# A transformer block in 3-term fp32r matmuls: the distances between the operands in SBUF are turned round

## The chip, the cores and the metric

The kernel runs on one core of one Trainium2 chip. The metric is the device time of one execution in microseconds (us), lower is better. The five engines of the core are called PE (matmul), with PEld for its weight loads, DVE (vector), ACT (scalar), POOL and SP; SP only issues transfers here.

SBUF, the memory that the engines work in, has 128 partitions; a tile has the same byte address in each of its partitions. A matmul on PE has two operands in SBUF: the weights, which are loaded into the array first and stay there, and the operand that then moves through it, column by column. This document calls *distance* the start address of the moving operand less the start address of the weights, taken modulo 256 bytes. A tile that lies "64 behind" another begins at an address 64 bytes higher, modulo 256.

## The reference: what is computed

One PixArt block on x of 16 x 256 x 256 (16 batches, 256 tokens, width 256), with 16 heads of width 16, a condition vector per batch and a context of 256 tokens per batch. Cut to what matters:

```python
shift_a, scale_a, gate_a, shift_m, scale_m, gate_m = split(silu(c) @ W_mod + b_mod, 6)
q, k, v = split(modulate(ln(x), shift_a, scale_a) @ W_qkv + b_qkv, 3)
x = x + gate_a * (softmax(q @ k.T * scale) @ v @ W_proj + b_proj)
q_c = ln(x) @ W_qc + b_qc
k_c, v_c = split(ln(context) @ W_kvc + b_kvc, 2)
x = x + softmax(q_c @ k_c.T * scale) @ v_c @ W_cproj + b_cproj
h = gelu(modulate(ln(x), shift_m, scale_m) @ W_mlp1 + b_mlp1)
x = x + gate_m * (h @ W_mlp2 + b_mlp2)
```

All inputs and the output are float32.

## The kernel before, in words

**Precision.** Nearly all products run in fp32r, a float32 read at reduced precision. So each factor is split into a high part and a rest, and a product is the sum of three matmuls: high by high, high by rest, rest by high. The two parts of a source stand in tiles `xTh` and `xTl` (four buffers each), those of the queries and keys in `qkh` and `qkl` before they are sent to their place.

**Units.** There are 32 units: a self attention and a cross attention for each batch. A unit makes its keys, queries and values, forms its scores, and projects the result. The heads of a unit stand in pairs, and `beat(n, k)` with k from 0 to 7 goes through one pair of heads for the unit n and, at the same time, for its neighbours. A beat calls `visit`, which issues

- `s_tile`: the scores of unit n+1 for the row maxima (tile `s`). The weights are 128 columns of the queries `u.q`, the moving operand is the keys `u.k`, 256 columns. DVE takes the maximum.
- `t_part`: the scores of unit n again, transposed (tile `st`). Here the weights are 128 columns of the keys and the moving operand is the queries. ACT takes the exponential of them.

Both run as pairs: one matmul on partitions 0 to 63 (0 to 62 for `s`), one on 64 to 127, side by side in the two halves of the array. The document calls such a half of the array a *lane*. Queries and keys of a unit lie in one tile `big` of which there are three, used in turn by the units; the queries come first, the keys `8 * N` floats and a gap of `APART` floats later.

**Projections between the scores.** `lane` and `lanes` fill each beat with twelve steps of two projections, one per lane: keys, queries, values or the output projection of other units. For keys and queries (`o.tok` false) the weights of the matmul are the weight matrix (`wself`, `wqc`, `wkc`) and the source `xT` moves; for values and output projections (`o.tok` true) the source stays and the matrix (`wtok`, `wvc`, `wcp`) moves.

**The product with the values** (`av_part`, tile `o`) is plain float32, four heads side by side in the columns of the array.

**The last stage.** After the units comes the MLP of 16 batches with matmuls over all 128 partitions: `mlp_first` and `mlp_ahead` (tile `ph`; weights W1 in `wself`, the source `xT..m` moves) and `mlp_second` (tiles `s` and `st`; the hidden `hh` or `hl`, in the buffers `qkh` and `qkl`, stays and W2, which takes the place of the third `big`, moves).

**What sets the order.** Every engine works in the program's order; the order is written out by hand in `beat` and in a table `E_` of steps and places. Transfers stand on SP's queue.

**Where tiles lie.** Two pools, `const` and `work`, lay tiles one behind the other as they are first named. A helper `gap(pool, n, name)` reserves n bytes that nothing uses, so that what is named after it moves up. These lines set the distances before:

```python
APART = 16
        if i == 2:
            gap(const, 64, "gap_w2")
wt = const.tile([P, 16 * H + 2 * APART], F32R, name="wself")
wtok = wt[:, 8 * H + 2 * APART:].rearrange("p (a h) -> p a h", h=H)
            if name == "k0":
                gap(work, 64, "gap_l")
```

Of the kernel before, what the change touches and what calls it, by code (L numbers as in the profile page):

```python
# [11 lines left out]
F32R = mybir.dt.float32r  # L12
# [4 lines left out]
P = 128  # L17
# [4 lines left out]
def pixart_block(  # L22
# [8 lines left out]
    B, N, H = x.shape  # L31
# [28 lines left out]
    const = ctx.enter_context(tc.tile_pool(name="const", bufs=1))  # L60
    work = ctx.enter_context(tc.tile_pool(name="work", bufs=2))
# [6 lines left out]
    def ps_gen(name, tag=None):  # L68


        if tag is None and ps_turn[0] is not None:
            ps_turn[0] ^= 1
            tag = (SHORT, LONG)[ps_turn[0]]
        tag = tag or SHORT
        return psum.tile([P, 512], F32, tag=tag, name=name, bufs=2)
# [9 lines left out]
    def gap(pool, n, name):  # L85

        pool.tile([P, n // 4], F32, tag=name, name=name, bufs=1)

    APART = 16
    big, qks = [], []  # L90
    for i in range(3):
        if i == 2:
            gap(const, 64, "gap_w2")
        t = const.tile([P, 16 * N + APART], F32R, name=f"big{i}")
        big.append(t[:, :16 * N].rearrange("p (s a n) -> p s a n", s=2, n=N))
        qks.append([t[:, c:c + 8 * N].rearrange("p (a n) -> p a n", n=N) for c in (0, 8 * N + APART)])
    vts = [const.tile([P, NT, NH, 32], F32, name=f"v{i}") for i in range(3)]
    wt = const.tile([P, 16 * H + 2 * APART], F32R, name="wself")
    wself = wt[:, :16 * H].rearrange("p (a h) -> p a h", h=H)
    wtok = wt[:, 8 * H + 2 * APART:].rearrange("p (a h) -> p a h", h=H)  # L100
    cb = const.tile([P, H], F32, name="cb")
    ones = cb[:8]
    DVE.memset(ones, 1.0)
# [266 lines left out]
    def transposed(src, name, scale=None, pool=False):  # L370

        o = Box()

        def place():
            o.ps = ps_gen(f"psT_{name}", SHORT)

        def turn(fs=range(KC)):
            if len(fs) == KC:
                place()
            for f in fs:  # L380
                for t in range(NT):
                    PE.transpose(o.ps[:, f * N + t * P:f * N + (t + 1) * P],
                                 src()[:, t, f * P:(f + 1) * P], ident)

        def high():
            hi = work.tile([P, KC, N], F32R, tag="xTh", name=f"xTh_{name}", bufs=4)
            lo = work.tile([P, KC, N], F32R, tag="xTl", name=f"xTl_{name}", bufs=4)
            o.xT = (hi, lo)
            if scale is None:
                ACT.copy(hi.rearrange("p k n -> p (k n)"), o.ps)  # L390
            else:
                for f in range(KC):
                    ACT.activation(hi[:, f], o.ps[:, f * N:(f + 1) * N], AF.Identity, scale=scale[f])

        def low():
            hi, lo = o.xT
            if scale is None:
                DVE.tensor_tensor(lo.rearrange("p k n -> p (k n)"), o.ps,
                                  hi.rearrange("p k n -> p (k n)"), ALU.subtract)
            else:  # L400
                for f in range(KC):
                    DVE.scalar_tensor_tensor(lo[:, f], o.ps[:, f * N:(f + 1) * N], scale[f],
                                             hi[:, f], ALU.mult, ALU.subtract)

        def full():
            o.y = work.tile([P, KC, N], F32, tag="y", name=f"y_{name}", bufs=1)
            if scale is None:
                ACT.copy(o.y.rearrange("p k n -> p (k n)"), o.ps)
            else:
                for f in range(KC):  # L410
                    ACT.activation(o.y[:, f], o.ps[:, f * N:(f + 1) * N], AF.Identity, scale=scale[f])

        def rest_pool():
            hi, lo = o.xT
            POOL.tensor_tensor(lo, o.y, hi, ALU.subtract)

        def low_pool():
            full()
            rest_pool()

        o.full, o.rest_pool, o.place = full, rest_pool, place
        o.parts = [turn, high, low]
        o.low_pool = low_pool
        o.turn, o.high, o.low = turn, high, low_pool if pool else low
        return o

    def mm3(dst, W, f, xT):

        n = 0
        for k in range(KC):  # L430
            for a, b in ((W[0], xT[0]), (W[0], xT[1]), (W[1], xT[0])):
                PE.matmul(dst, a[:, k, f * P:(f + 1) * P], b[:, k],
                          start=(n == 0), stop=(n == 3 * KC - 1))
                n += 1
# [40 lines left out]
    def to_stack(W, src, bias, dst, which, name):  # L475

        o = Box()
        lo_row = (2, 1)[which]  # L480

        o.W, o.src, o.tok, o.name = W, src, False, name

        def first():
            o.ps = ps_gen(f"ps_{name}", LONG)
            mm3(o.ps[:, 0:N], W, 0, src.xT)

        def third():
            mm3(o.ps[:, N:], W, 1, src.xT)

        def second():
            third()
            high()

        def high():
            o.hi = work.tile([P, KC, N], F32R, tag="qkh", name=f"h_{name}", bufs=3)
            for f in range(KC):
                ACT.activation(o.hi[:, f], o.ps[:, f * N:(f + 1) * N], AF.Identity, bias=bias[f])

        def low():  # L500
            if name == "k0":
                gap(work, 64, "gap_l")
            o.lo = work.tile([P, KC, N], F32R, tag="qkl", name=f"l_{name}", bufs=3)
            if name == "k0":
                gap(work, 192, "gap_mx")
            for f in range(KC):
                DVE.scalar_tensor_tensor(o.lo[:, f], o.ps[:, f * N:(f + 1) * N], bias[f], o.hi[:, f],
                                         ALU.add, ALU.subtract)

        def low_pool():  # L510
            o.lo = work.tile([P, KC, N], F32R, tag="qkl", name=f"l_{name}", bufs=3)
            y = work.tile([P, KC, N], F32, tag="y", name=f"y_{name}", bufs=1)
            for f in range(KC):
                ACT.activation(y[:, f], o.ps[:, f * N:(f + 1) * N], AF.Identity, bias=bias[f])
            POOL.tensor_tensor(o.lo, y, o.hi, ALU.subtract)

        def send(part, q=SP):

            row = (0, 3 - lo_row, lo_row)[part]
            q.dma_start(dst[row:row + 4 * 31 + 1:4].bitcast(F32), (o.hi if part < 2 else o.lo).bitcast(F32))  # L520

        o.send = send
        o.parts = [first, second, low]
        o.third = third
        o.low_pool = low_pool
        o.high, o.low = high, low
        o.send_high = lambda: [send(part) for part in range(2)]
        o.send_low = lambda: send(2)
        o.steps = [first, second]
        return o  # L530
# [799 lines left out]
```

## Time and profile before

| | |
|---|---|
| median of 3 runs | 729.45 us (729.22 to 731.1) |
| the profiled execution | 729.69 us |
| its span, from the first to the last instruction | 727.9 us |
| PE busy | 716.5 us (98%), 9007 matmuls |
| PEld busy | 594.5 us (82%) |
| DVE, ACT, POOL busy | 558.7, 556.6, 540.9 us (77, 76, 74%) |
| granted TensorE clock | 0.999 |

A matmul's recorded duration holds its way through the array, so that matmuls that follow each other overlap in time: a group's mean is 276 to 306 ns while the next one starts much sooner. What a matmul costs in a full stream is the time from its start to the start of the next one in its lane, its *pace*. It is read from the timeline. Both lanes together make a *slot*: two half-height matmuls or one over all partitions.

### The profile page before, as it was taken

The page shows a single profiled execution, that of the slowest core. Times are in us where ns is not written, and L with a number is a line of the kernel's source. Part 1 is how long each engine was busy: PE and PEld are TensorE (multiplying, and loading weights), DVE is VectorE, ACT ScalarE, POOL GpSimd, SP SyncE. Part 2 cuts the span into 40 slices and gives each one's busy share as a digit, 9 for nine tenths or more (in the row PEclk, how much of TensorE's full clock was granted, in tenths as well). Part 3 has the DMA queues.
Part 4 walks back from the last instruction along what each step waited for, and adds up shares of the span by engine and source line. Part 5 has one row for each costly group of instructions (what it writes and reads, how often), then busy time and mean ns, then how long its engine had stood idle before and what let it go on. Part 6 is the DMA issues. An engine that isn't in the chain of part 4 may idle for free.

```text
span 727.9 us, 22489 instructions
## 1 busy us (share of the span) xinstructions
PE 716.5 (98%) x9007; PEld 594.5 (82%) x9007; DVE 558.7 (77%) x876; ACT 556.6 (76%) x971; POOL 540.9 (74%) x533
## 2 busy tenths in 40 slices
PE   9999999999999999999999999999999999999997
PEld 8777777777777777777777787777679999999996
DVE  4878888788888888888878888778675777777743
ACT  5667888888888888888888888888767677666661
POOL 8455687887867777786786798998766888666561
PEclk9999999999999999999999999999999999999999
DMA  7364545545545555454546655455332322312122
GB/s 251 139 232 154 171 150 179 170 162 176 180 144 169 173 185 173 170 185 135 183 162 190 191 180 200 150 176 196 92 90 89 89 59 87 71 62 88 49 53 73
DMA packets 81388, 106.14 MB, mean 146 GB/s; under 512 B 16451, under 2 KB 44389, under 8 KB 81285
## 3 DMA queue, kind: packets, MB, share of 16 engines
q1 hardware_dynamic: 80180, 103.92, 43.7%
q8 instruction: 71, 1.16, 0.7%
q10 hardware_dynamic: 1104, 0.79, 0.4%
q14 instruction: 33, 0.26, 0.1%
HBM read 35.89 MB, written 8.98 MB: 62 GB/s over the span
## 4 chain that ended last, share of the span: by engine, by line
PE 90%; DMA 4%; DVE 3%; ACT 1%; issue 1%; POOL 1%; SPq 0%; ACTq 0%
PE s L51 17%; PE o L51 16%; PE st L51 14%; PE ph L51 12%; PE ps_q L51 4%; PE ps_kc L51 3%; PE ps_qc L51 3%; PE ps_k L51 3%; PE ps_v_c L51 3%; PE ps_P_s L51 3%; PE ps_v_s L51 2%; PE ps_P_c L51 2%; DVE mx L51 2%; PE psT_c L51 2%; PE psT_s L51 1%; PE psT_q L51 1%
## 5 line engine op out<-in xcount | busy, mean ns | idle before, releaser
L51 DVE TENSOR_REDUCE mx<-s 128x4 f32<-128x1024 f32 x252 | 307.8, 1221 | 88.7 <-PE s L51 85.4
L51 ACT ACTIVATE pt<-st 128x1024 f32<-128x1024 f32 x256 | 263.2, 1028 | 53.8 <-PE st L51 52.6
L51 PE MATMUL o<-pt,v 128*32 128x256 f32 x2048 | 137.0, 385 | 0.0
L51 PE MATMUL s<-big 63*128 63x256 f32 x1008 | 117.5, 306 | 2.2 <-DMA U_s<-oT 0.8
L51 PE MATMUL st<-big 64*128 64x256 f32 (+1 forms) x1040 | 108.3, 283 | 1.4 <-ACT pt L51 0.7
L51 PE MATMUL ph<-xTh_m,wself 128*128 128x256 f32 x512 | 99.5, 280 | 0.0
L51 PEld LDWEIGHTS s<-big 63*128 63x128 f32 x1008 | 77.6, 185 | 21.8 <-issue 9.1
L51 POOL TENSOR_TENSOR hl<-hf,hh 128x512 fp32r<-128x512 f32 x60 | 81.2, 1370 | 18.8 <-ACT hh L51 18.8
L51 PEld LDWEIGHTS st<-big 64*128 64x128 f32 (+1 forms) x1040 | 81.5, 186 | 4.8 <-ACT pt L51 2.1
L51 PEld LDWEIGHTS o<-pt,v 128*32 128x32 f32 x2048 | 53.4, 109 | 38.9
L51 PEld LDWEIGHTS ph<-xTh_m,wself 128*128 128x128 f32 x512 | 81.8, 188 | 1.2 <-issue 0.4
L51 PE MATMUL ph<-xTl_m,wself 128*128 128x256 f32 x256 | 70.9, 277 | 0.0
L51 ACT ACTIVATE hf<-ph,bT 128x256 f32<-128x256 f32 x112 | 47.1, 475 | 19.4 <-PE ph L51 19.2
L51 ACT ACTIVATE hh<-ph,bT 128x256 fp32r<-128x256 f32 x112 | 47.2, 477 | 18.9 <-PE st L51 8.0
L51 PEld LDWEIGHTS ph<-xTl_m,wself 128*128 128x128 f32 x256 | 48.2, 188 | 0.0
L51 PE MATMUL s<-big,hh 128*128 128x256 f32 x256 | 45.2, 277 | 0.0
L51 DVE TENSOR_SCALAR xn_m<-x,mv_m,rs_m 128x256 f32<-128x256 f32 x28 | 33.9, 1249 | 14.8 <-POOL rs_m L51 14.8
L51 POOL TENSOR_SCALAR xn_c<-c,mv_c,rs_c 128x256 f32<-128x256 f32 x32 | 38.9, 1226 | 1.7
L51 PE MATMUL st<-big,hh 128*128 128x256 f32 x224 | 39.5, 276 | 0.0
L51 POOL TENSOR_SCALAR xn_q<-x,mv_q,rs_q 128x256 f32<-128x256 f32 x31 | 37.7, 1226 | 1.7
L51 PEld LDWEIGHTS s<-big,hh 128*128 128x128 f32 x256 | 38.7, 188 | 0.0
L51 ACT COPY oT<-o 128x512 f32<-128x512 f32 x64 | 37.6, 587 | 1.4 <-PE o L51 1.4
(226 smaller groups left out, 2119.1 us busy)
## 6 DMA issues: line engine op xcount, KB each, us to landing
big<-h_kc SPq DMA_DIRECT2D x32, 256.0 KB
big<-h_qc SPq DMA_DIRECT2D x32, 256.0 KB
big<-h_k SPq DMA_DIRECT2D x31, 256.0 KB
big<-h_q SPq DMA_DIRECT2D x31, 256.0 KB
big<-l_k SPq DMA_DIRECT2D x16, 256.0 KB
big<-l_q SPq DMA_DIRECT2D x16, 256.0 KB
g<-gd SPq DMA_DIRECT2D x16, 256.0 KB
U_s<-oT SPq DMA_DIRECT2D x32, 128.0 KB
```

What stands on the lines that cost most here:

```text
L51: i = f(*a, **k)
```

## The change

Five places change, and all of them move tiles in SBUF; no instruction is added, taken away or moved. The two built programs have the same 12412 instructions, in the same order on every engine, with the same shapes and the same waits.

```diff
-    APART = 16
+    APART = 48
     for i in range(3):
         if i == 2:
-            gap(const, 64, "gap_w2")
+            gap(const, 192, "gap_w2")
         t = const.tile([P, 16 * N + APART], F32R, name=f"big{i}")
...
-    wt = const.tile([P, 16 * H + 2 * APART], F32R, name="wself")
+    wt = const.tile([P, 16 * H + 32], F32R, name="wself")
-    wtok = wt[:, 8 * H + 2 * APART:].rearrange("p (a h) -> p a h", h=H)
+    wtok = wt[:, 8 * H + 32:].rearrange("p (a h) -> p a h", h=H)
...
         def high():
+            if name == "s0":
+                gap(work, 128, "gap_x")
             hi = work.tile([P, KC, N], F32R, tag="xTh", name=f"xTh_{name}", bufs=4)
...
             if name == "k0":
-                gap(work, 64, "gap_l")
+                gap(work, 192, "gap_l")
```

The start addresses modulo 256, as both programs have them:

| tile | before | after |
|---|---|---|
| queries of `big` 0, 1, 2 | 160, 224, 96 | 160, 96, 224 |
| keys of `big` 0, 1, 2 | 224, 32, 160 | 96, 32, 160 |
| W2 (in `big` 2) | 96 | 224 |
| sources `xTh`, `xTl` | 96 | 224 |
| `wself` (W of self keys and queries, W1), `wqc`, `wkc` | 160 | 160 |
| `wtok` (W of self values and projection), `wvc`, `wcp` | 32 | 32 |
| `qkh`, `qkl` (hidden of the MLP) | 160 | 160 |
| exponentials `pt`; values `v` | 96; 160 and 32 | 96; 160 and 32 |

So the distances (moving less weights) become:

| matmuls | before | after |
|---|---|---|
| keys, queries, W1 (source moves) | 192 | 64 |
| values, output projections (matrix moves) | 192 | 64 |
| W2 (matrix moves) | 192 | 64 |
| `st` (queries move, keys stay) | 192 | 64 |
| `s` (keys move, queries stay) | 64 | 192 |
| `o` and the transposes | | as before |

Every tile that a matmul of fp32r reads begins at 32 modulo 64, before and after.

## The prediction

> **What bounds the kernel now.** I read the first page from the top, then the chain, then the groups with their shapes kept apart, and last the timeline. The page first:
>
> ```profile
> span 727.9 us, 22489 instructions
> PE 716.5 (98%) x9007; PEld 594.5 (82%) x9007; DVE 558.7 (77%) x876; ACT 556.6 (76%) x971; POOL 540.9 (74%) x533
> ...
> PEclk9999999999999999999999999999999999999999
> ...
> PE 90%; DMA 4%; DVE 3%; ACT 1%; issue 1%; POOL 1%; SPq 0%; ACTq 0%
> PE s L51 17%; PE o L51 16%; PE st L51 14%; PE ph L51 12%; PE ps_q L51 4%; PE ps_kc L51 3%; PE ps_qc L51 3%; PE ps_k L51 3%; PE ps_v_c L51 3%; PE ps_P_s L51 3%; PE ps_v_s L51 2%; PE ps_P_c L51 2%; DVE mx L51 2%; PE psT_c L51 2%; PE psT_s L51 1%; PE psT_q L51 1%
> ```
>
> PE is the bound at a full clock, and 90% of the chain that ended last is PE's. Of that the product `o` and the transposes (`psT`) are outside the change; the rest are fp32r matmuls whose distances turn. In the answer for waits, PE waits for nobody for long:
>
> ```profile
> PE s L51 <- DMA U_s<-oT: 0.8, 1, 0.8
> PE st L51 <- ACT pt L51: 0.7, 3, 0.4
> ```
>
> DVE and ACT wait for PE instead (last columns of the first two rows here, which come from the groups by shape; columns: busy us, mean ns of one, idle before and its releaser):
>
> ```profile
> L51 DVE TENSOR_REDUCE mx<-s 128x4 f32<-128x1024 f32 x252 | 307.8, 1221 | 88.7 <-PE s L51 85.4
> L51 ACT ACTIVATE pt<-st 128x1024 f32<-128x1024 f32 x256 | 263.2, 1028 | 53.8 <-PE st L51 52.6 <-POOL wself L51 0.9
> L51 PE MATMUL s<-big 63*128 63x256 f32 x1008 | 117.5, 306 | 2.2 <-DMA U_s<-oT 0.8 <-DVE mx L51 0.7
> L51 PE MATMUL st<-big 64*128 64x256 f32 x1024 | 106.3, 282 | 0.7 <-ACT pt L51 0.7
> L51 PE MATMUL ph<-xTh_m,wself 128*128 128x256 f32 x512 | 99.5, 280 | 0.0
> L51 PE MATMUL ph<-xTl_m,wself 128*128 128x256 f32 x256 | 70.9, 277 | 0.0
> L51 PE MATMUL s<-big,hh 128*128 128x256 f32 x256 | 45.2, 277 | 0.0
> L51 PE MATMUL ps_P_s<-wself,xTh_as 64*128 64x256 f32 x256 | 35.0, 276 | 0.0
> ...
> L51 PE MATMUL ps_P_c<-wcph,xTl_ac 64*128 64x256 f32 x96 | 14.8, 274 | 0.0
> ```
>
> So a nanosecond on the pace of a matmul is a nanosecond on the end. The pace of today, from the timeline (start, duration, what). First full-height matmuls of the MLP, then the two lanes of a beat; the lanes' rows between first and last left out:
>
> ```profile
> 640.00 0.39 PE L51 MATMUL ph<-xTh_m,wself 128*128 128x256 f32 x2
> ...
> 641.02 0.28 PE L51 MATMUL ph<-xTh_m,wself 128*128 128x256 f32 x1
> ```
>
> ```profile
> 327.76 0.28 PE L51 MATMUL ps_P_c<-wcph,xTh_ac 64*128 64x256 f32 x1
> 327.76 0.28 PE L51 MATMUL ps_qc<-xTh_q,wqch 64*128 64x256 f32 x1
> ...
> 329.04 0.28 PE L51 MATMUL ps_qc<-xTl_q,wqch 64*128 64x256 f32 x1
> 329.06 0.28 PE L51 MATMUL ps_P_c<-wcph,xTl_ac 64*128 64x256 f32 x1
> ```
>
> Nine full-height matmuls start between 640.00 and 641.02: 1.02 / 9 = 113.3 ns each. In the lanes eleven intervals lie between first and last: 1.28 / 11 = 116.4 ns (`ps_qc`) and 1.30 / 11 = 118.2 ns (`ps_P_c`). All are at a distance of 192. The lanes carry 3 to 5 ns that the full-height stream doesn't.
>
> **The change part by part.** Five places, one effect: start addresses. The programs have the same instructions, order and waits, so no step, transfer or wait is added, and nothing is queued behind anything new.
>
> *Who reads the moved tiles.* ACT, DVE and POOL write and read `xT` and the queries and keys at other addresses, and SP's transfers fill `big`. Each of these tiles begins at 32 modulo 64 before and after, so I cost it at nothing. These engines have idle time before them that PE ended (the first two rows above), and PE's longest wait for a transfer is 0.8 us, so a few nanoseconds on each would be covered; without that cover each nanosecond on the 256 exponentials or 252 maxima would cost a quarter of a microsecond.
>
> *What PE reads.* While a matmul streams, the weights of the next one are loaded, so two reads of SBUF run side by side, and the change alters how their addresses stand to each other: 192 to 64 in most, 64 to 192 in `s`. How many slots:
>
> - full height, 192 to 64: `ph` 512 + 256, W2 on `s` 256 + 128 and on `st` 224 + 112 + 48: 1536 slots;
> - lanes of projections, 192 to 64: twenty groups from `ps_P_s` (256) to `ps_P_c` (96), whose first and last rows stand above, hold 2808 matmuls, two to a slot: 1404;
> - `st`, 192 to 64: 1024 / 2 = 512;
> - `s`, 64 to 192: 1008 / 2 = 504.
>
> About a hundred more in set-up and tail are left out. Net 1536 + 1404 + 512 - 504 = 2948 slots go from 192 to 64.
>
> What a slot pays, the trace shows in one place only: `s` runs at 64 today and `st` at 192, next to each other, in the same lanes and of the same size. From the answer for the tile `big` (minimum/median/maximum ns):
>
> ```profile
> L51 PEld LDWEIGHTS st<-big x1040: 182/186/190, 21.2 to 544.9; 64*128 64x128 f32 x171, 63*128 63x128 f32 x3
> L51 PE MATMUL st<-big x1040: 271/278/391, 21.3 to 545.0; 64*128 64x256 f32 x171, 63*128 63x256 f32 x3
> L51 PEld LDWEIGHTS s<-big x1008: 182/186/189, 23.3 to 527.7; 63*128 63x128 f32 x168
> L51 PE MATMUL s<-big x1008: 271/279/389, 23.3 to 527.9; 63*128 63x256 f32 x168
> L51 PEld LDWEIGHTS s<-big,hh x256: 187/188/192, 551.9 to 716.5; 128*128 128x128 f32 x128
> L51 PE MATMUL s<-big,hh x256: 276/276/281, 552.1 to 716.6; 128*128 128x256 f32 x128
> ```
>
> And from the chain in order of time (start, length), two visits without a wait ahead of `s`:
>
> ```profile
> 325.41 0.24 PE s L51 x4
> 325.65 0.23 PE st L51 x4
> ...
> 329.33 0.24 PE s L51 x4
> 329.57 0.23 PE st L51 x4
> ```
>
> The medians of the matmuls differ by 1 ns (279 against 278), those of the weight loads by nothing. In the chain two slots of `s` take 0.24 us and two of `st` 0.23: 5 ns a slot, at a resolution of as much. (The means, 306 and 282, can't be used: many `s` stand first after a wait.) So 64 costs 1 to 5 ns more than 192 where the trace shows both. I take 1.5 ns, near the medians, because they hold a thousand matmuls each. Sum: 2948 x 1.5 = +4.4 us on 729.69, 734.1 us. The profiled execution stands 0.24 us above the median of the runs, less than their spread.
>
> *Bounds.* Upwards: the shortest and longest loads of a full-height matmul are 187 and 192 with a median of 188, so one disturbance more shows as about 4 ns. One in each slot: 2948 x 4 = +11.8 us, 741.5 us. Downwards: the full-height stream has no more to gain than its pace of 113.3 shows of waste, and that is unseen, so I take none; the lanes and `st` could lose 116.4 and 118.2 less 113.3, on average 4 ns, in 1404 + 512 slots: -7.7 us, 722.0 us.
>
> **A page that speaks against a cost.** The rows say that a load beside a stream of another phase costs between 0 and 5 ns. The Trainium skill, "SBUF — State Buffer", section "SBUF: two separate sides", says that of the compute engines only VectorE and GpSimd contend, for a port pair that they share, and that PE never waits for anyone at SBUF; "TensorE: Matmul & The Clock Gate", Part 2, says that PE has two independent read ports and that loading the next weights takes no bandwidth from the running matmul. By that rule addresses don't matter and the sum would be 729.7 instead of 734.1 us. It is the first rival below. No row here compares a full-height stream at two distances, so the trace neither confirms nor refutes it for the larger half.
>
> **The rivals.**
>
> *Nothing happens: 729.7 us.* The two read streams don't touch each other; distance is without effect. For it: equal medians of the loads (186 and 186). Two full-height matmuls in a row already read 1024 bytes beside 512, so the two addresses drift past each other several times whatever their start. Against it: the 1 to 5 ns between `s` and `st`.
>
> *Faster: 725.9 us.* The 3 to 5 ns that lanes carry over full height come from the distance of 192, where the load begins close ahead of the stream, and 64 takes them away. Half of the bound: -3.8 us. For it: something does disturb the lanes, and full height shows 113.3 is possible. Against it: full height runs at the same 192 without the loss, so the second lane is the likelier cause, and that stays. It decides if the lanes come below 115 ns and full height stays at 113.
>
> *One more disturbance in every slot: 741.5 us*, the upper bound above. For it: durations come in steps (188, then 192), so an effect may come as a whole step rather than as 1.5 ns. Against it: `s` at 64 has the same extremes (182 and 189) as `st` at 192 (182 and 190).
>
> **How the numbers follow.** Forecast, a small loss (0.5 to 2.5 ns a slot, 731.2 to 737.1 us): 0.33. A whole step: 0.24. Nothing: 0.20. Faster: 0.23. About 0.3% (2.2 us) is what a measurement tells from no change; 0.03 of the forecast falls within it. So slower 0.54, same 0.23, faster 0.23. The range for 8 in 10 reaches from 724.0, half-way between the faster case and the lower bound, to the whole step, 741.5.
>
> **What would show it.** Forecast: the nine `ph` starts take 1.03 to 1.04 us instead of 1.02, the median of `ph` rises from 276 by 1 or 2 ns, and in the visits `s` and `st` change places (0.23 and 0.24). A whole step: the nine take 1.05 or more and loads of 191 to 192 become the rule. Nothing: every median within 1 ns. Faster: `ps_P_c` and `ps_qc` at 113 to 115 ns. The slots from 560 us on are all full height; a difference there is the first thing to read. I am wrong altogether if full height becomes faster than 113 ns.

## The result, and the profile after

The changed kernel takes 735.76 us (median of 4 runs, 734.6 to 736.57) against 729.34 us before: a ratio of 1.0081 with a 95% interval of 1.0058 to 1.0104. The forecast was 734.1 us in a range of 724.0 to 741.5. The profiled execution of the changed kernel is the slowest of its four, 736.57 us with a span of 734.8 us.

The page of the changed kernel, from its top and its chain:

```profile
span 734.8 us, 22489 instructions
...
PE 723.9 (99%) x9007; PEld 602.3 (82%) x9007; DVE 559.6 (76%) x876; ACT 558.5 (76%) x971; POOL 541.0 (74%) x533
...
PE 94%; DVE 3%; DMA 1%; ACT 1%; issue 1%; SPq 0%; POOL 0%; ACTq 0%
```

The span is 6.9 us longer and PE's busy time 7.4 us. The busy times of DVE and ACT rise by 0.9 and 1.9 us, which is far less than the loss, and that of POOL by 0.1. The loss is PE's own.

The product `o` exists only in the units, and its first and last start cut the span into set-up, units and rest. From the answer for that tile, before and after (duration minimum/median/maximum in ns, then first and last start in us):

```profile
L51 PE MATMUL o<-pt,v x2048: 379/379/404, 39.8 to 548.8; 128*32 128x256 f32 x187
```

```profile
L51 PE MATMUL o<-pt,v x2048: 379/379/404, 41.5 to 550.8; 128*32 128x256 f32 x187
```

| stage | before | after | difference |
|---|---|---|---|
| up to the first `o` | 39.8 us | 41.5 us | +1.7 |
| units, first to last `o` | 509.0 | 509.3 | +0.3 |
| the rest, nearly all MLP | 179.1 | 184.0 | +4.9 |

The set-up's part comes with a lower granted clock at the start: the first 60 us have 0.97 after and 1.00 before. Here are those two windows (PE, PEld, DVE, ACT, POOL busy, clock, DMA share, GB/s), before and after:

```profile
0.00:60.00 60.00, 56.62 (x548) 46.69 (x549) 40.24 (x77) 37.76 (x64) 36.17 (x46) 1.00 0.59 197
```

```profile
0.00:60.00 60.00, 56.33 (x537) 46.21 (x538) 39.10 (x76) 36.85 (x63) 36.28 (x46) 0.97 0.59 197
```

A clock lower by 0.03 over 60 us is worth 1.8 us, an estimate from these two rows, and as much as the whole difference of 1.7. Two of the experiments below with the same mean clock of 0.996 over the span (`full_128` with 41.6 us to the first `o`, `full_32` with 40.5) began late as well; but `hh_moved` took 40.9 us to its first `o` with a clock of 1.00 in this window, so the clock is not all of it. I don't count this part as the change's, and no run isolates it. The MLP is where the time went. Its matmuls, from the answers for `ph` (first before, then after) and, after the change, for `big`:

```profile
L51 PE MATMUL ph<-xTh_m,wself x512: 276/276/387, 516.0 to 711.3; 128*128 128x256 f32 x171
```

```profile
L51 PE MATMUL ph<-xTh_m,wself x512: 276/279/392, 517.8 to 718.1; 128*128 128x256 f32 x171
```

```profile
L51 PEld LDWEIGHTS st<-big x1040: 182/186/190, 21.5 to 546.9; 64*128 64x128 f32 x171, 63*128 63x128 f32 x3
L51 PE MATMUL st<-big x1040: 271/279/389, 21.5 to 547.0; 64*128 64x256 f32 x171, 63*128 63x256 f32 x3
...
L51 PEld LDWEIGHTS s<-big,hh x256: 187/187/189, 554.0 to 723.5; 128*128 128x128 f32 x128
L51 PE MATMUL s<-big,hh x256: 279/279/284, 554.1 to 723.7; 128*128 128x256 f32 x128
```

And the timeline in the MLP, to be read against the rows at 640 us of the prediction:

```profile
646.79 0.28 PE L51 MATMUL ph<-xTh_m,wself 128*128 128x256 f32 x1
...
648.09 0.28 PE L51 MATMUL ph<-xTh_m,wself 128*128 128x256 f32 x1
```

Eleven matmuls start between these two rows: 1.30 / 11 = 118.2 ns, where it was 113.3. The median duration of `s<-big,hh` went from 276 to 279 ns, while the weight loads stayed (188, now 187): it is the stream that lost, and the record of the load doesn't show it.

I also took the start-to-start times of all matmuls in a running stream (from the start times in the trace, same lane, intervals of 105 to 130 ns that follow one of at most 130). Their means:

| stream | before | after | distance |
|---|---|---|---|
| `ph` to `ph`, full height | 113.8 ns | 117.6 ns | 192 to 64 |
| `s<-big,hh` to itself | 114.0 | 117.5 | 192 to 64 |
| keys and queries, lanes | 115.5 | 117.2 | 192 to 64 |
| values and projections, lanes | 115.8 | 117.6 | 192 to 64 |
| `st` to `st` | 119.6 | 121.7 | 192 to 64 |
| `s` to `s` | 121.5 | 119.5 | 64 to 192 |

Every stream that went from 192 to 64 became slower, the one that went the other way became faster.

### The profile page after: what moved, and what is told of

Read it like the earlier page. It is cut to its first block, busy times and chain, and to the rows that moved or that the text cites. A ratio compares the mean times of both kernels' runs of the same rounds, so it can differ in the third digit from the quotient of the medians.

```text
span 734.8 us, 22489 instructions
## 1 busy us (share of the span) xinstructions
PE 723.9 (99%) x9007; PEld 602.3 (82%) x9007; DVE 559.6 (76%) x876; ACT 558.5 (76%) x971; POOL 541.0 (74%) x533
## 4 chain that ended last, share of the span: by engine, by line
PE 94%; DVE 3%; DMA 1%; ACT 1%; issue 1%; SPq 0%; POOL 0%; ACTq 0%
PE s L51 19%; PE o L51 16%; PE st L51 15%; PE ph L51 12%; PE ps_k L51 4%; PE ps_qc L51 4%; PE ps_q L51 3%; PE ps_kc L51 3%; PE ps_v_c L51 3%; PE ps_P_s L51 3%; PE ps_v_s L51 3%; PE ps_P_c L51 2%; PE psT_c L51 2%; DVE mx L51 2%; PE psT_s L51 2%; PE psT_q L51 1%
## 5 line engine op out<-in xcount | busy, mean ns | idle before, releaser
L51 ACT ACTIVATE pt<-st 128x1024 f32<-128x1024 f32 x256 | 263.2, 1028 | 52.7 <-PE st L51 51.5
L51 PE MATMUL ph<-xTh_m,wself 128*128 128x256 f32 x512 | 102.2, 283 | 0.0
```

The lines of the kernel that those rows point to most:

```text
L51: i = f(*a, **k)
```

## The experiments

**The parts alone.** Three kernels take the change apart. `w2_only` moves W2 to 64 and leaves all else. Its edit, with a gap that keeps what lies behind at the same place modulo 256:

```diff
-            gap(const, 64, "gap_w2")
+            gap(const, 192, "gap_w2")
+    gap(const, 128, "gap_v")
     vts = [const.tile([P, NT, NH, 32], F32, name=f"v{i}") for i in range(3)]
```

> W2 alone at a distance of 64, everything else as before (the third tile of queries and keys moves with it, its inner distances stay at 64 and 192). Theory: each full-height matmul whose distance is 64 pays about 4 ns on its pace, 113.6 to 117.7 ns; 768 matmuls with W2, so +3.1 us, 732.4 us, and the MLP's ph stays at its median of 276 ns while the matmuls with hh and hl go from 276 to 280. Rival, the loss hangs on the place of the sources (who writes and reads xT): no change, 729.3 us, every median 276.

`src_only` moves the sources alone:

```diff
+            if name == "s0":
+                gap(work, 128, "gap_x")
...
-                gap(work, 64, "gap_l")
+                gap(work, 192, "gap_l")
```

> The sources alone 128 bytes further (distance 64 for keys, queries, values, projections and W1), queries, keys and W2 as before. Theory, all slots count: ph 768 x 4 ns = 3.1 us and 1404 slots of projections x 1.7 ns = 2.4 us, 734.8 us. Rival, the units hide their slots behind other waits (the stage of the units was only 0.3 us longer in the changed kernel): ph alone counts, +3.1 us, 732.4 us.

`keys_only` turns queries and keys alone, with W2 held at its place:

```diff
-    APART = 16
+    APART = 48
+    gap(const, 128, "gap_v")
...
-    wt = const.tile([P, 16 * H + 2 * APART], F32R, name="wself")
+    wt = const.tile([P, 16 * H + 32], F32R, name="wself")
-    wtok = wt[:, 8 * H + 2 * APART:].rearrange("p (a h) -> p a h", h=H)
+    wtok = wt[:, 8 * H + 32:].rearrange("p (a h) -> p a h", h=H)
```

> Keys 192 behind queries (s at 192, st at 64) alone; sources and W2 at 192 as before. Theory, all slots count and the units were only 0.3 us longer because the visits gave back what the projections lost: between s and st and at their seams 1.5 to 2 us are won, 727.6 us, faster than both kernels. Rival, s and st trade places evenly (2.0 ns less in 252 pairs of slots, 2.1 ns more in 256): no change, 729.3 us.

| kernel | ratio, 95% interval | median | up to first `o` | units | rest |
|---|---|---|---|---|---|
| `w2_only` | 1.0065, 1.004 to 1.0091 | 735.09 us | 40.5 us | 508.2 | 184.2 |
| `src_only` | 1.0073, 1.0044 to 1.0102 | 735.88 | 40.1 | 510.0 | 183.9 |
| `keys_only` | 0.9998, 0.9967 to 1.0028 | 730.13 | 39.9 | 507.9 | 179.4 |
| all three (the change) | 1.0081, 1.0058 to 1.0104 | 735.76 | 41.5 | 509.3 | 184.0 |

The rival of `w2_only`, no change, is out: 735.09 us. Once W2 is in its place PE alone reads it, so what other engines do with the moved tiles isn't needed for the loss. `src_only` lost 1.0 us in the units, where its theory had 2.4 and its rival nothing, so neither held there; the MLP lost 4.8 us against the 3.1 of both.

The parts don't add up, and that is the finding. W2 alone costs the MLP 5.1 us, the sources alone 4.8, both together 4.9. `w2_only` was to cost 3.1 us by "each slot for itself"; the interval's lower end, 0.4%, is 2.9 us, but the trace settles it, because `ph` lost as much as W2 although both operands of `ph` still stand at 192. First `ph` and `hh` of `w2_only`, then `hh` of `src_only`, whose W2 stands at 192:

```profile
L51 PE MATMUL ph<-xTh_m,wself x512: 276/281/387, 516.0 to 716.1; 128*128 128x256 f32 x171
```

```profile
L51 PE MATMUL s<-big,hh x256: 279/280/284, 552.0 to 721.7; 128*128 128x256 f32 x128
```

```profile
L51 PE MATMUL s<-big,hh x256: 276/281/286, 553.3 to 722.9; 128*128 128x256 f32 x128
```

So the pace is not a price that each matmul pays for its own operands. In one kernel, `w2_only`, the same matmul with the same operands at the same distance of 192 runs at both paces. Two stretches of its timeline:

```profile
558.69 0.28 PE L51 MATMUL ph<-xTl_m,wself 128*128 128x256 f32 x1
...
559.83 0.28 PE L51 MATMUL ph<-xTh_m,wself 128*128 128x256 f32 x1
...
591.72 0.28 PE L51 MATMUL ph<-xTh_m,wself 128*128 128x256 f32 x1
...
593.01 0.28 PE L51 MATMUL ph<-xTh_m,wself 128*128 128x256 f32 x1
```

Ten starts in 1.14 us are 114 ns; eleven in 1.29 us are 117.3 ns. The kernel before has this too, at the end of its units, where every full-height matmul stands at 192. Here twelve `psP_c` run fast and the `ph` behind them slow, all at 192:

```profile
536.31 0.28 PE L51 MATMUL psP_c<-wcpl,xTh_ac 128*128 128x256 f32 x1
...
537.44 0.28 PE L51 MATMUL psP_c<-wcph,xTl_ac 128*128 128x256 f32 x1
537.56 0.28 PE L51 MATMUL ph<-xTh_m,wself 128*128 128x256 f32 x1
...
538.85 0.28 PE L51 MATMUL ph<-xTh_m,wself 128*128 128x256 f32 x1
```

Ten starts in 1.13 us (113 ns), then eleven in 1.29 us (117.3 ns). The load of the first `ph`'s weights starts with the last `psP_c`, at 537.44 us. There the matrix that moves starts at 32 and the weights that are being loaded at 160, so at this seam the distance to the next weights is 128, not 192. That is a hint at what ends the faster pace, and no proof. A stream of full-height matmuls has a faster pace near 113 ns and a slower one near 118; once at one, it keeps it over many matmuls. From the first matmul with `hh` on, the share of start-to-start times of at most 115 ns (of those below 130, without those of the transposes) is 92% before and in `keys_only`, 0.1% in the changed kernel, 7% in `w2_only` and 4% in `src_only`.

`keys_only` was to win 1.5 to 2 us by the theory and nothing by its rival. Its profile shows the units 1.1 us shorter, its times show nothing, so it ran again in five rounds:

> The same kernel as keys_only, in five rounds, since three left it open whether s at 192 and st at 64 win anything (ratio 0.9998, interval 0.9967 to 1.0028, while its profile had the units 1.0 us shorter than before). Theory, the seams around s win a microsecond: ratio 0.9985, 728.3 us against 729.4. Rival, nothing: ratio 1.000.

The ratio is 0.9993, interval 0.9977 to 1.0009 (729.86 against 729.85 us). The medians are equal, but the interval holds the theory's 0.9985 too, so a gain of a microsecond is not excluded. The second profile didn't repeat the first one's: its units take 508.9 us, 0.1 less than before, where the first had 507.9. So the length of a stage in a single profile is good to about 1 us, and this version isn't shown to beat the kernel before.

**One of three, two of three.** In each W2 term two matmuls have `hh` as weights and one `hl`. `rest_moved` puts `hl` alone at 64, `hh_moved` puts `hh` alone there:

```diff
-                gap(work, 64, "gap_l")
+                gap(work, 192, "gap_l")
...
-                gap(work, 192, "gap_mx")
+                gap(work, 64, "gap_mx")
```

> The rests qkl moved by 128 bytes alone, so that of the three matmuls hh by W2 high, hh by W2 rest, hl by W2 high only the weights hl lie elsewhere (address 32 instead of 160). Theory, the load of the NEXT weights disturbs the running stream: the slow one is the second with hh, under which hl is loaded; half of the hh matmuls last 280 instead of 276 ns, the mean of hh about 278, hl stays at 276. Rival, a matmul's own weights count: hh stays at 276, hl goes to 280. Either way 256 slots x 4 ns, about +1 us.

```diff
-    gap(work, 64, "gap_h")
+    gap(work, 192, "gap_h")
...
-    gap(work, 192, "gap_pt")
+    gap(work, 64, "gap_pt")
```

> The high parts qkh moved by 128 bytes alone, so that in the MLP two of the three matmuls of each W2 term stand at a distance of 64 and the one with hl at 192; all else as before. Theory, the pace is a state of the stream that each matmul pushes one way or the other, and the majority decides: W2 runs at about 117.7 ns and drags ph along for much of the MLP, +3 to +5 us, near 733 us; the median of ph between 276 and 280. Rival, each matmul pays for itself: only 512 slots pay 4 ns, +2.0 us, ph stays at 276 throughout.

`rest_moved`: 729.71 us, no loss, and the medians of `hh` and `hl` stay at 276. Both answers that I had offered were wrong: a third of the matmuls at 64 does nothing at all, whichever of the two weights is to blame. So this run couldn't tell the next weights from a matmul's own, and that stays open. `hh_moved`: 730.74 us, with 729.68 before on the same chip; its span is 1.0 us longer than the profiled one of before. But that microsecond doesn't lie in the MLP: the first `o` starts at 40.9 us instead of 39.8, the units are 0.4 us shorter, and the rest takes 179.4 us, 0.3 longer. So neither the 3 to 5 us of the theory nor the 2.0 of the rival were lost, and the majority didn't decide either. 86% of its intervals in the MLP are at most 115 ns. One stretch is slow as a whole, `ph` at 192 included: the 96 full-height matmuls between the transposes at 606.0 us and those at 617.8 have a mean pace of 118.4 ns, the stretches just before and behind it 113.4. Two pieces, one of this stretch and one of a later one:

```profile
612.12 0.28 PE L51 MATMUL ph<-xTh_m,wself 128*128 128x256 f32 x1
...
613.42 0.28 PE L51 MATMUL ph<-xTh_m,wself 128*128 128x256 f32 x1
...
700.36 0.28 PE L51 MATMUL ph<-xTh_m,wself 128*128 128x256 f32 x1
...
701.60 0.28 PE L51 MATMUL ph<-xTh_m,wself 128*128 128x256 f32 x1
```

1.30 / 11 = 118.2 ns in the first, 1.24 / 11 = 112.7 ns in the second. What remains of the theory, as far as these runs go: the pace is a state; a distance of 192 lets the fast one last; matmuls at 64 can push a stream out of it, and not each of them does.

**Other distances.** Sources and W2 together at five more distances, everything else as before (the third tile of queries and keys moves along with W2, its inner distances stay). The edit of `full_0`; the others differ from it only in the sizes of these gaps:

```diff
-            gap(const, 64, "gap_w2")
+            gap(const, 128, "gap_w2")
+    gap(const, 192, "gap_v")
...
+            if name == "s0":
+                gap(work, 64, "gap_x")
...
-            if name == "k0":
-                gap(work, 64, "gap_l")
```

> Sources and W2 at a distance of 0 (keys, queries and W1 at 0 in the lanes, values and projections at 128), s and st as before. Theory, only the two signs differ, and equal starts are the worst case, since stream and load begin in the same place: the MLP at 117.7 ns or slower, 735 us or more. Rival, nothing but the sign of the distance modulo 256 counts and 0 is as good as 192: 729 us, MLP matmuls at 276.

> Sources and W2 at a distance of 32, so that they begin at a multiple of 64 while the weights that stay begin at 32 modulo 64 (lanes: keys, queries 32, values and projections 96), s and st as before. Theory, the step comes with distances between 0 and 64: MLP at 117.7 ns, 735 us. Rival, a start at a multiple of 64 saves the stream a piece of a line whatever the distance: MLP at 110 ns or less, below 726 us.

> Sources and W2 at a distance of 128 (keys, queries and W1 at 128 in the lanes, values and projections at 0), s and st as before. Theory, the load may begin anywhere behind the stream but not ahead of it within 64 bytes; 128 is then like 192: 729 us, MLP at 113.4 ns. Rival, half way round is as bad as 64: MLP at 117.7 ns, 735 us.

> Sources and W2 at a distance of 160 (lanes: keys, queries 160, values and projections 224), s and st as before; one step of 32 bytes from 192 towards 128, where the pace was 118.6 ns. Theory, as for 224: between 113.5 and 118.6 ns, 730 to 736 us. Rival, 192 is the edge of a good region that reaches to 160: MLP at 113 ns, the lanes below 115, 726 us or less.

> Sources and W2 at a distance of 224 (lanes: keys, queries 224, values and projections 160), s and st as before; one step of 32 bytes from 192 towards 0, where the pace was 120 ns. Theory, the stream must begin well behind the weights, and 192 is the one good place among the multiples of 64 with room on both sides: 224 lies between 192 and 0, MLP between 113.5 and 120 ns, 730 to 736 us. Rival, a small lag is better still: MLP at 113 ns and the lanes below 115, 726 us or less.

| distance in the MLP | time | median duration of `ph<-xTh_m` | pace of `ph` | last `o` to the end |
|---|---|---|---|---|
| 0 | 739.9 us | 283 ns | 119.8 ns | 186.9 us |
| 32 | 735.79 | 280 | 117.0 | 183.4 |
| 64 (the change) | 735.76 | 279 | 117.6 | 184.0 |
| 128 | 740.2 | 281 | 118.7 | 185.2 |
| 160 | 736.97 | 281 | 118.2 | 185.0 |
| 192 (before) | 729.34 | 276 | 113.8 | 179.1 |
| 224 | 736.92 | 282 | 118.3 | 184.9 |

The row of 64 is the change itself, which turns `s` and `st` as well. The rows of `full_0` and of `full_160`:

```profile
L51 PE MATMUL ph<-xTh_m,wself x512: 274/283/388, 517.9 to 721.3; 128*128 128x256 f32 x171
```

```profile
L51 PE MATMUL ph<-xTh_m,wself x512: 277/281/387, 517.1 to 718.3; 128*128 128x256 f32 x171
```

Among the seven tried, 192 is the only good one: 32 bytes to either side of it the gain is gone. The theories of `full_0` and `full_32` held (that equal starts are the worst holds for the pace; by time `full_128` is 0.3 us worse), those of `full_160` and `full_224` in the pace (their times lie 1 us above what was given); the theory of `full_128` (as good as 192) was wrong and its rival right. The rival of `full_32`, that a start at a multiple of 64 saves something, is out. In the lanes it is the same: keys and queries run at 115.5 ns at 192 and at 119.4, 117.1, 117.2, 118.9, 118.0 and 118.1 at 0, 32, 64, 128, 160 and 224. Values and projections, in the other lane, run at 115.8 ns at 192 and at 119.1, 119.8, 117.6, 118.6, 118.2 and 118.2 at 0, 96, 64, 128, 160 and 224. This bears on a rival: that the start of one operand counts by itself. In the lanes it is out. For values and projections the moving matrix starts at 32 in every kernel of the table and only the sources, the weights there, move; yet at the distances that both kinds have, they are within 0.4 ns of keys and queries. And in `full_32` the same sources serve lanes that run at 117.1 and 119.8 ns. In the MLP this stays open: the weights start at 160 in all the kernels of the table, and `rest_moved` and `hh_moved`, which moved weights instead, lost next to nothing. Each of these five was run once, so their order among themselves (735.8 to 740.2 us) is less sure than the gap to 192.

## Why the prediction was right, and where it was wrong

The sign, the range and the size came out (734.1 forecast, 735.76 measured). Step by step:

- *PE is the bound, a nanosecond of pace is one of the end.* Right in the MLP. In the units only in part: the projections gave up 2.2 us in one lane and 1.8 in the other (sums of their start-to-start times between the first and the last `o`), the matmuls and seams around `s` and `st` gave 1.9 and 1.4 us back, and 0.3 us remained. Not all of this came from `s` with its new distance: in `src_only`, whose `s` and `st` stand as before, the same sums are +1.6 and +2.1 us for the projections and 0.6 and 1.1 us given back. All of them are from one profile each.
- *The other engines cost nothing.* Right: the mean of ACT's exponential stayed at 1028 ns and that of DVE's maximum went from 1221 to 1222.
- *The price from `s` against `st`, 1.5 ns a slot.* The sign was right, and the two did change places (119.6 to 121.7 and 121.5 to 119.5 ns); in the chain's rounded 0.23 and 0.24 us only part of this shows. In `keys_only`, which turns these two alone, `st` stands at 120.9 and `s` at 120.2 ns. But the pace of `st` is no clean measure of its own distance: it is 120.8 to 121.4 ns in `w2_only`, `full_0`, `full_160` and `full_224` too, where that distance is still 192. The cleanest place for `s` is right behind transposes: from its first to its second matmul in a lane the median there is 226 ns before and in `src_only`, and 222 and 221 in the changed kernel and in `keys_only`. The size was wrong where most of the time is: 3.8 ns in `ph` and 3.5 in `hh`, nearly the whole step that I had as a rival. In the lanes it was 1.7 to 1.8. By the prediction's own signs the MLP took the whole step: nine starts of `ph` now take 9 x 118.2 = 1.06 us, where the forecast had 1.03 to 1.04 and the whole step 1.05 or more. But the loads of 191 to 192 that were to come with it did not become the rule (median 187).
- *The sum.* It is near by luck, because errors cancel. The 1536 full-height slots at 1.5 ns were to cost 2.3 us, and the rest, which holds most of them, became 4.9 us longer. The 1404 + 512 - 504 slots of the units were to cost 2.1 us and cost 0.3. The 1.7 us of the set-up were not foreseen; as the runs of the changed kernel lie between 734.6 and 736.57, the change itself may be nearer to 734.6.
- *A sum over slots at all.* This was the wrong picture. W2 alone and the sources alone cost the MLP 5.1 and 4.8 us, and both together 4.9, since the stream as a whole is fast or slow.
- *Nothing happens.* Out: all the seven distances of the table but one cost 6 us or more. The prediction had taken from the Trainium skill, "SBUF — State Buffer", section "SBUF: two separate sides", that PE never waits for anyone at SBUF, and by that addresses would not matter. They do: where PE's two operands start moves PE's pace from 113.8 to as much as 119.8 ns, with no other change in the program. Whether the two reads meet at SBUF or elsewhere no run shows.
- *Faster.* Out: the lanes lost too.

## What to carry to other kernels

Two tiles that a matmul stream reads side by side are worth placing on purpose: here the start of the moving operand 192 bytes past that of the weights, modulo 256, was worth 6 to 11 us of 730 against each of six other distances, five of them run once, with no instruction changed. Look for it in the start-to-start times of a full stream and not in the busy share, which read 98 and 99%. And don't add up such effects slot by slot: change one operand alone and look at the neighbours that were not touched.

## What the runs showed that I had not expected

A stream of equal matmuls has states that last. At the same distance and with the same operands it ran at 113 and at 117 to 118 ns within one execution, for ten and more matmuls at a time, in the kernel before as well as in `w2_only` and `hh_moved`. It can hold from one group of transposes in the MLP to the next, 96 matmuls: before, such stretches run at 113.4 to 113.5 ns, in the changed kernel at 117.8, in `full_0` at 120.0. In `full_160` some run at 117.3 and others at 118.7 ns, all with the same distance, so there are more states than two. A third of W2's matmuls at the bad distance cost nothing (729.71 us). Two thirds cost the MLP 0.3 us, no more than two profiles of one kernel differ there (179.4 and 178.7 us in `keys_only` and its repeat). All of them cost 5 us and took the untouched `ph` along. What sets the state at the start of a stream, and whether the next weights or a matmul's own disturb it, was not found; nor, for the MLP, whether it is the distance or the start of the moving operand that counts; nor was it tried whether 256 bytes is the right period for what is called distance here.
